# Block transposes on VectorE and a regroup through DRAM in place of crossbar transposes, in a linear-attention and FP4 feed-forward layer

## Chip, core and metric

The kernel runs on one core of a Trainium2 chip. The time is device microseconds of that core for one launch; the reported figure is the median of 3 runs. The core has five engines with instruction queues of their own: TensorE (PE in the profile, with its weight loads as PEld), VectorE (DVE), ScalarE (ACT), GpSimd (POOL) and SyncE (SP), which here only issues DMAs. Each queue runs its instructions in order, and an instruction waits at the head of its queue until what it needs is there.

## The reference

One layer over x of shape (16, 512, 256), all in float32. First attention without a softmax over the sequence, with 16 heads of 16 features, then a gated feed-forward whose inputs and weights are quantised to FP4 in blocks of 16 and dequantised again. Both halves end with a residual and a LayerNorm.

```python
def features(x):                       # per head, last dim
    p = exp(x - max(x)); return p / (sum(p) + 1e-6)
q, k = features(x @ Wq + bq), features(x @ Wk + bk); v = x @ Wv + bv
context = (q @ k.T / (sum(q) + 1e-6)) @ v          # per batch and head
x = layernorm(x + context @ Wo + bo)

def fp4(x):                            # blocks of 16 along the last dim
    scale = maximum(max(abs(x)) / 6, 1e-12)
    return GRID[searchsorted(MID, abs(x / scale))] * sign(x) * scale
gate, up = fp4(x) @ fp4(w_gate).T, fp4(x) @ fp4(w_up).T       # w_gate, w_up: (704, 256)
x = layernorm(x + fp4(silu(gate) * up) @ fp4(w_down).T)       # w_down: (256, 704)
```

Since nothing but a division stands between q @ k.T and v, the kernel computes k.T @ v per batch, multiplies it with Wo to a 256x256 matrix M, and takes q @ M.

## The kernel before

P is 128, D is 256, FF is 704. A batch has four tiles of 128 tokens, taken as two pairs; there are 32 pairs. The body does not run its work as it is written. Every operation is entered in a `Plan` with an engine, a time, a due time and the buffers it reads and writes; `Plan.order` then simulates the engines and gives one order, and the instructions are issued in it. So the order on each queue comes from the planner's times (`t_pe`, `t_dve`, `t_act`, `t_pool`, lines 245 to 262, and for a DMA an issue time of 0.45 us unless told otherwise), from the due times (in units of PAIR = 25) and from the number of buffers of each tag. On the chip, each queue keeps that order whatever the real times are.

The work of a batch, in order:

- `load_x` (371) loads x. `split_x` (743), from batch 2 (EARLY) on, also loads x transposed: a crossbar DMA transposes the batch as 16-bit halves (748) into `xTr`, and four DMAs regroup it into planes `xpl` (754).
- `project` (758) gets xT of a pair either by four TensorE transposes and a ScalarE copy out of PSUM (`transposed`, 625, lines 632 and 635, batches 0 and 1) or by two ScalarE copies that join the 16-bit planes (`join`, 776). Then q and k (783) and v (793) are multiplied, VectorE adds the biases (786, 799) and takes the maxima (805), GpSimd subtracts them (809).
- `features` (813): exp on ScalarE (820), sums and reciprocals on VectorE (822 to 833), the product on GpSimd (839).
- `key_values` (843): k.T v (852) and M (866).
- `attend` (878): q is transposed by TensorE (632), the product with M (894), residual and LayerNorm (`norm`, 685), the result x1 to DRAM (905).

The second half works on pairs:

- `quantise` (909) loads x1 (912), `codes` (638) makes 16-bit codes `xc` and scales `ns_x` on VectorE and ScalarE (650 to 663). A crossbar DMA on the SP queue transposes the codes (923) into `xcT`. `spread_scales` (667) transposes the scales by TensorE (672), copies them (674), writes them to DRAM by a DMA on ScalarE's queue (677) and reads them back on the SP queue so that every partition has the scale of its block of 16 (681). GpSimd multiplies both to `xqT` (928).
- `gate_up` (932): per tile, gate and up in two halves of 352 columns (948), silu on ScalarE (953), the product on VectorE (955), `codes` again, then for the pair a crossbar DMA of the codes `hc` (987), `spread_scales`, and GpSimd's products into `hq` (991). The columns of `w_guT` are laid out with the last 64 rows twice, so that the two tiles of a pair share the middle of eleven groups of 128. The last pair is dequantised by VectorE and transposed by TensorE instead (960 to 985).
- `down` (995): six products of 256 columns per tile (1005), residual, LayerNorm, output.

Every float32 product is two instructions in the profile, a transpose is one. The buffers that hold `hq` and the spread scales of h ("big") are two. `weight_scales` and `fp4_exact` (476, 518) quantise the weights, spread between the first batches; `transpose_gate_up` and `transpose_down` (568, 593) transpose them by TensorE. `due_at` (1019) puts the first half LEAD = 11 batches ahead of the second: the first gate of pair 0 is due when the attention of eleven batches is.

## Time and profile before

| what | us |
|---|---|
| median of 3 runs | 796.67 (795.27 to 798.91) |
| the profiled execution | 797.62 |
| its span, first to last instruction | 795.9 |
| ScalarE busy with the joins of x (L776, 56 of 0.762) | 39.1 |
| ScalarE busy with copies of scales (L674, 63) | 16.2 |
| GpSimd busy with products into hq (L991, 31 of 1.658 and 31 of 1.421) | 95.4 |
| GpSimd busy with products into xqT (L928, 32 of 1.168) | 37.4 |
| GpSimd waiting for the read of h's scales before L991 | 114.4 |

TensorE's granted clock is 0.996 over the span. The DMA engines moved 100.68 MB in 141884 packets, 95069 of them under 512 bytes. Of the time of 16 DMA engines, SP's queue (q1) took 55.3%, ScalarE's (q10) 7.5%. The landing times of DMAs are not given for this run, so they are read from the instruction that waited for one.

The times in these views are of one execution. "Busy" of an engine is the union of its instructions' spans; the times of lines can overlap a little. In the timeline, the columns are start, length, engine, line, operation, tile written and tile read, and the number of instructions merged; a queue's name ends in q. An issue of a DMA is the time that its queue is held, not the transfer.

### The profile page before, as it was taken

To read this page: it belongs to the slowest core of one execution; us is meant where nothing else is said; L and a number is where in the kernel's file an instruction comes from. 1 tells how busy PE (TensorE), PEld (TensorE's weight loads), DVE (VectorE), ACT (ScalarE), POOL (GpSimd) and SP (SyncE) were. 2 spreads that over 40 slices of the span, in tenths; PEclk is the share of its full clock that TensorE was granted. 3 is DMA by queue.
4 is the path that set the end of the run, shared out by engine and by line. 5 is a ranking of instruction groups with operands and counts; after the bars stand their busy time and mean duration, and the time that the engine had idled before them with its cause. 6 is when DMAs were issued, how large, how long until landed. Compare 5 with 4: busy or idle time off the path is not lost.

```text
span 795.9 us, 10225 instructions
## 1 busy us (share of the span) xinstructions
PE 770.2 (97%) x3134; PEld 550.4 (69%) x3134; DVE 589.4 (74%) x1194; ACT 441.5 (55%) x978; POOL 413.4 (52%) x510
## 2 busy tenths in 40 slices
PE   7999999998989999999999999999999999999996
PEld 4575766675766767777777777777777777677775
DVE  3979988887788798677666776776776776776663
ACT  1385786756879976545555444444444444444432
POOL 3488886978798766554533333343343343343331
PEclk9999999999999999999999999999999999999999
DMA  9536463434343243594374978977977977977721
GB/s 271 129 97 180 126 167 90 124 98 132 92 133 93 67 116 90 133 117 114 89 132 137 131 145 140 140 136 139 144 135 139 139 138 139 143 141 140 132 70 41
DMA packets 141884, 100.68 MB, mean 126 GB/s; under 512 B 95069, under 2 KB 125317, under 8 KB 141829
## 3 DMA queue, kind: packets, MB, share of 16 engines
q1 hardware_dynamic: 123464, 80.53, 55.3%
q10 hardware_dynamic: 18365, 19.49, 7.5%
q8 instruction: 25, 0.41, 0.2%
q14 instruction: 30, 0.25, 0.1%
HBM read 51.25 MB, written 18.70 MB: 88 GB/s over the span
## 4 chain that ended last, share of the span: by engine, by line
PE 83%; DVE 10%; ACT 3%; DMA 2%; POOL 1%; issue 1%; POOLq 0%; SPq 0%; DVEq 0%; ACTq 0%
PE bank L948 37%; PE bank L1005 20%; PE bank L783 10%; PE bank L894 6%; PE bank L793 4%; PE bank L852 2%; DVE fs L822 2%; PE bank L866 1%; PE bank L632 1%; DVE qk L786 1%; DVE mx L805 1%; DVE fr L833 1%; DMA x<-dx 1%; PE bank L672 1%; ACT qk L820 1%
## 5 line engine op out<-in xcount | busy, mean ns | idle before, releaser
L948 PE MATMUL bank<-w_guT,xqT 128*128 128x352 f32 x1024 | 310.6, 459 | 0.0
L948 PEld LDWEIGHTS bank<-w_guT,xqT 128*128 128x128 f32 x1024 | 193.9, 190 | 101.9 <-issue 1.4
L1005 PE MATMUL bank<-w_dT,hq 128*128 128x256 f32 x768 | 174.3, 379 | 0.6 <-DVE r L695 0.6
L991 POOL TENSOR_TENSOR hq<-hcT,hq 128x768 f32<-128x768 bf16 (+1 forms) x62 | 94.1, 1539 | 133.1 <-DMA hq<-d_h 114.4
L1005 PEld LDWEIGHTS bank<-w_dT,hq 128*128 128x128 f32 x768 | 141.9, 190 | 25.2 <-issue 4.2
L955 DVE TENSOR_TENSOR h<-bank,g 128x352 f32<-128x352 f32 x128 | 66.7, 522 | 93.0 <-PE bank L948 53.5
L783 PE MATMUL bank<-w_qkv,xT 128*128 128x512 f32 x256 | 123.4, 611 | 6.2 <-DVE qk L786 3.1
L953 ACT ACTIVATE g<-bank 128x352 f32<-128x352 f32 x128 | 58.6, 460 | 96.7 <-PE bank L948 94.4
L809 POOL TENSOR_TENSOR qk<-qk,mx 128x512 f32<-128x512 f32 x64 | 67.5, 1077 | 31.9 <-DVE mx L805 31.8
L783 PEld LDWEIGHTS bank<-w_qkv,xT 128*128 128x128 f32 x256 | 47.7, 196 | 48.5 <-issue 33.8
L839 POOL TENSOR_TENSOR qk<-qk,fr 128x512 f32<-128x512 f32 x64 | 66.5, 1067 | 23.2 <-DVE fr L833 12.1
L661 ACT ACTIVATE sq<-h,magic 128x704 f32<-128x704 uint16 x64 | 56.4, 881 | 29.2 <-DVE h L658 28.3
L723 POOL TENSOR_SCALAR var_d<-var_d 128x2 f32<-128x2 f32 x31 | 5.9, 191 | 120.6 <-ACT y L719 120.5
L786 DVE TENSOR_TENSOR qk<-bank,b_qkv 128x512 f32<-128x512 f32 x64 | 43.4, 682 | 32.4 <-PE bank L783 31.9
L793 PE MATMUL bank<-w_qkv,xT 128*128 128x256 f32 x256 | 60.7, 380 | 1.6 <-DVE v L799 1.2
L894 PE MATMUL bank<-M,qT 128*128 128x256 f32 x256 | 59.8, 381 | 1.5 <-ACT M L872 1.3
L793 PEld LDWEIGHTS bank<-w_qkv,xT 128*128 128x128 f32 x256 | 48.0, 190 | 16.7 <-issue 8.1
L650 DVE TENSOR_REDUCE bank<-h 128x44 f32<-128x704 f32 x64 | 57.3, 895 | 2.0
L658 DVE SCALAR_TENSOR_TENSOR h<-h,bank 128x704 f32<-128x704 f32 x64 | 56.7, 886 | 2.1
L894 PEld LDWEIGHTS bank<-M,qT 128*128 128x128 f32 x256 | 48.2, 190 | 13.7 <-issue 3.4
L887 POOL TENSOR_TENSOR xb<-x,b_o 128x512 f32<-128x512 f32 x32 | 41.0, 1284 | 20.8 <-DVE r L710 20.2
L674 ACT COPY sT_h<-bank 88x128 f32<-88x128 f32 x31 | 8.1, 260 | 73.6 <-PE bank L672 65.0
(139 smaller groups left out, 1081.5 us busy)
## 6 DMA issues: line engine op xcount, KB each, us to landing
hq<-d_h SPq DMA_DIRECT2D x31, 704.0 KB
dx<-x1n ACTq DMA_DIRECT2D x32, 256.0 KB
x<-dx SPq DMA_DIRECT2D x32, 256.0 KB
xs<-d_x SPq DMA_DIRECT2D x32, 256.0 KB
out_dram<-y ACTq DMA_DIRECT2D x31, 256.0 KB
x<-_attn_hidden_states_dram SPq DMA_DIRECT2D x15, 512.0 KB
xpl<-xTr SPq DMA_DIRECT2D x56, 128.0 KB
d_h<-sT_h ACTq DMA_DIRECT2D x31, 44.0 KB
```

The costliest lines, as they stand in the source:

```text
L650: op("DVE", t_dve(n), due, lambda: nc.vector.tensor_reduce(amax[:, g], b3(src()), AX.X, ALU.max, apply_absolute_value=True), ins=[src_b], ...
L658: op("DVE", t_dve(n), due, lambda: nc.vector.scalar_tensor_tensor(b3(xn()), b3(src()), TIE * UP / BIG, bcast(inv[:, g], BLK), ALU.mult, AL ...
L783: op("PE", t_pe(D2), due, lambda c=c, u=u, pqk=pqk: nc.tensor.matmul(pqk.tile, xT[:, 2 * c + u, :], w_qkv[:, c, :D2], start=c == 0, stop=c ...
L793: nc.tensor.matmul(pv[:, u * D : (u + 1) * D], xT[:, 2 * c + u, :], w_qkv[:, c, D2:], start=c == 0, stop=c == DC - 1,)
L809: op("POOL", t_pool(D2), due, lambda g=g: nc.gpsimd.tensor_tensor(qk3()[:, g, :], qk3()[:, g, :], bcast(mx[:, g], HD), ALU.subtract), ins= ...
L839: nc.gpsimd.tensor_tensor(f3, f3, bcast(r[:, t * 2 * H : (t + 1) * 2 * H], HD), ALU.mult)
L894: nc.tensor.matmul(pu(pa.tile)[:, u, :], qT[:, 2 * u + c, :], M[:, c, :], start=c == 0, stop=c == DC - 1,)
L948: op("PE", t_pe(F2), due + u * 0.2 * PAIR, lambda c=c, u=u, lo=lo, ps_=ps_: nc.tensor.matmul(ps_[:, :F2], xqT[:, 2 * u + c, :], w_guT[:, c ...
L953: op("ACT", t_act(F2), due, lambda g=g, pg=pg: nc.scalar.activation(g.tile, pg[:, :F2], AF.Silu), ins=[pg], outs=[g], table="silu")
L955: op("DVE", t_dve(F2), due, lambda g=g, h=h, pu_=pu_, k=k: nc.vector.tensor_tensor(h[:, k * F2 : (k + 1) * F2], pu_[:, :F2], g.tile, ALU.m ...
L991: op("POOL", t_pool((gs.stop - gs.start) * P), d, lambda gs=gs: nc.gpsimd.tensor_tensor(part(1)[:, gs, :], hcT[:, gs, :], part(0)[:, gs, : ...
L1005: op("PE", t_pe(D), due, lambda f=f, g=g, u=u: nc.tensor.matmul(pu(pd.tile)[:, u, :], part(1)[:, g, :], w_dT[:, f + u * (f == NR), :], sta ...
```

## The change

- **Codes.** Before, one crossbar DMA turns codes of 128 tokens by n into their transpose. After, two neighbouring 16-bit codes are taken as one 32-bit word, VectorE transposes blocks of 32 by 32 words, one write puts the tile into DRAM and four reads, one for each 32 partitions, bring the blocks back so that a partition holds two neighbouring features for all tokens (`regroup`). All five DMAs are on the SP queue. Even and odd features lie side by side, so `w_guT` and `w_dT` are transposed from every second column, and GpSimd reads every second code. h has its codes padded from 704 to 768 per tile, in two fixed slots that are cleared at the start.
- **Scales.** VectorE transposes them in blocks of 32, four DMAs on the SP queue write them, one reads them back for every partition. TensorE's transposes, ScalarE's copies and the writes on ScalarE's queue go.
- **x.** TensorE transposes x in all batches; `split_x` and the joins go.
- **Order.** LEAD is 10; x has four buffers and its loads are all due six intervals ahead; weights are due one interval earlier, those of `w_down` two; gates from pair 2 on wait for `w_dT`. The last pair's route is the same with a layout of its own (12 transposes instead of 11). The maxima and reciprocals for x have one slot each instead of two.

```diff
-LEAD = 11
-
-EARLY = 2
+LEAD = 10
+
+FIRST = 2
...
-    FX = FF + TR
+    TG = -(-FF // (2 * P))
+    LW = FF // 2 - (TG - 1) * P
+    HB = 2 * P // BLK
...
-    places = {"amx": [0, 0], "ivx": [2 * D // BLK * 2, 0], "amh": [2 * D // BLK * 4, 0]}
-    places["ivh"] = [places["amh"][0] + 2 * FF // BLK * 2, 0]
+    slots, places = {"amx": 1, "ivx": 1, "amh": 2, "ivh": 2, "ivd": 1}, {}
+    for tag, k in slots.items():
+        places[tag] = [sum(slots[t] * 2 * (D if t[2] == "x" else FF) // BLK for t in places), 0]
...
+    nsh = const.tile([P, 2, 2 * TG * HB], F32, name="nsh")
+    hcs = const.tile([P, 2, 2 * TG * 2 * P], U16, name="hcs")
...
-        x = buf([TPB, D], "x", 3, f"x_{b}")
+        x = buf([TPB, D], "x", 4, f"x_{b}")
...
-    w_guT = const.tile([P, DC, 2 * FX], F32, name="w_guT")
-
-    w_dT = const.tile([P, NR + 2, D], F32, name="w_dT")
+    w_guT = const.tile([P, DC, 2 * FF], F32, name="w_guT")
+
+    w_dT = const.tile([P, 2 * TG, D], F32, name="w_dT")
...
+        nc.gpsimd.memset(nsh, 0.0)
+        nc.gpsimd.memset(hcs, 0.0)
...
-                        nc.tensor.transpose(pt[:, j, :], gu_rows()[:, r, cols], ident)
+                        nc.tensor.transpose(pt[:, j, :], gu_rows()[:, r, c::2], ident)
...
+                        at = 2 * P * g + t
+                        nc.tensor.transpose(pt[:n, 2 * t + c, :], dn_rows()[:, c, at : at + 2 * n - 1 : 2], ident)
...
-    def spread_scales(nscale, nb, dst, tag, name, due, holds=()):
-
-        n = P // BLK
-        pt = psum("pt", f"ps{name}")
-        sT = buf([P], "sT" + tag, 2, f"sT_{name}")
-        op("PE", t_pe(P) / 2, due, lambda: nc.tensor.transpose(pt[:nb, 0, :], nscale[:, :nb], ident),
-           ins=[nscale], outs=[pt], holds=[sT])
-        op("ACT", t_act(P) + 0.05, due, lambda: nc.scalar.copy(sT[:nb, :], pt[:nb, 0, :]), ins=[pt], outs=[sT])
-
-        d = Buf(dr, [n, nb // n, P], "d" + tag, 3, f"d_{name}")
-        dma(f"w{name}", 4.0, due, lambda: nc.scalar.dma_start(d.tile.rearrange("b g t -> g b t"), sT[:nb, :]),
-            ins=[sT], outs=[d], queue="ACT")
+    def regroup(src, dst, n, tag, name, due):
+
+
+        d = Buf(dr, [P, 4, n], "g" + tag, 3, f"g_{name}", U32)
+        dma(f"g{name}", 3.0, due, lambda: nc.sync.dma_start(d.tile, src.tile), ins=[src], outs=[d])
+
+        def back():
+            rows = d.tile.rearrange("(a i) q n -> i a q n", i=32)
+            for q in range(4):
+                nc.sync.dma_start(dst[32 * q : 32 * q + 32, :, :], rows[:, :, q, :])
+
+        dma(f"h{name}", 3.5, due, back, ins=[d], outs=[dst], issue=1.8)
+
+    def spread_scales(nscale, G, dst, tag, name, due, holds=()):
+
+
+        n = P // 8
+
+        sT = buf([G, 32], "sT" + tag, 2, f"sT_{name}")
+        op("DVE", 0.15 + 32 * G / 960.0, due, lambda: nc.vector.transpose(
+            sT.tile.rearrange("p g (r u) -> p g r u", u=2),
+            nscale.tile.rearrange("p (u g r) -> p g r u", u=2, r=n),
+        ), ins=[nscale], outs=[sT], port=True)
+        d = Buf(dr, [2 * n, G, P], "d" + tag, 3, f"d_{name}")
+
+        def write():
+            for a in range(0, P, 32):
+                nc.sync.dma_start(d[:, :, a : a + 32], sT[a : a + 32, :, :])
+
+        dma(f"w{name}", 4.0, due, write, ins=[sT], outs=[d], issue=1.8)
         into, dst_b = dst
 
-        dma(f"r{name}", 4.0 + nb * 0.08, due, lambda: nc.sync.dma_start(
-            into(), d.tile.rearrange("b g t -> b (g t)").unsqueeze(1).to_broadcast([n, BLK, nb // n * P])),
+        dma(f"r{name}", 3.0 + 0.7 * G, due, lambda: nc.sync.dma_start(
+            into(), d.tile.rearrange("(r u) g t -> r (u g t)", u=2).unsqueeze(1).to_broadcast([n, 8, 2 * G * P])),
             ins=[d], outs=[dst_b], holds=holds)
...
-    def split_x(b, due):
-
-
-        t = buf([2 * DC, L], "xTr", 1, f"xTr_{b}", U16)
-        pl = planes[b] = buf([2, DC, L], "xpl", 1, f"xpl_{b}", U16)
-        dma(f"xt{b}", 8.0, due, lambda: nc.sync.dma_start_transpose(t.tile, hidden[b].bitcast(U16)),
-            outs=[t], issue=5.0)
-
-        def regroup():
-            for h in range(2):
-                for g in range(2):
-                    nc.sync.dma_start(pl[g * P // 2 : (g + 1) * P // 2, h, :, :], t[h:P:2, g::2, :])
-
-        dma(f"xg{b}", 4.0, due, regroup, ins=[t], outs=[pl], issue=1.8)
...
-        if b < EARLY:
-            xT = transposed(
-                lambda: [x[:, 2 * p + u, cc * P : (cc + 1) * P] for cc in range(DC) for u in range(2)],
-                "xT", f"xT_{n}", due, [x if b else (x, p)],
-            )
-        else:
-            xT, pl = buf([2 * DC, P], "xT", 2, f"xT_{n}"), planes[b]
-
-            def join():
-                for h in range(2):
-                    half = xT.tile.bitcast(U16).rearrange("p (c u) (n t) -> p c (u n) t", c=DC, t=2)[:, :, :, h]
-                    nc.scalar.copy(half, pl[:, h, :, p * 2 * P : (p + 1) * 2 * P])
-
-            op("ACT", 2 * (0.16 + 2 * D / 975.0), due, join, ins=[pl], outs=[xT], name="join")
+        xT = transposed(
+            lambda: [x[:, 2 * p + u, cc * P : (cc + 1) * P] for cc in range(DC) for u in range(2)],
+            "xT", f"xT_{n}", due, [x if b else (x, p)],
+        )
...
-        xcT = buf([G, P], "xcT", 2, f"xcT_{i}", BF16)
-        dma(f"xT{i}", 4.0, due, lambda: nc.sync.dma_start_transpose(xcT.tile, xc.tile.bitcast(BF16)),
-            ins=[xc], outs=[xcT], issue=1.2)
-        xs_ = buf([G, P], "xs", 2, f"xs_{i}")
-        xqT = buf([G, P], "xqT", 2, f"xqT_{i}")
-        spread_scales(scales[1], n // BLK, (lambda: xs_.tile.rearrange("p g t -> p (g t)"), xs_), "x", f"x{i}", due, [xqT])
-        op("POOL", t_pool(n), due, lambda: nc.gpsimd.tensor_tensor(xqT.tile, xcT.tile, xs_.tile, ALU.mult),
-           ins=[xcT, xs_], outs=[xqT])
+        xw, xcT = (buf([4, 2 * 32], t, 2, f"{t}_{i}", U32) for t in ("xw", "xcT"))
+        op("DVE", 0.15 + n / 2 / 960.0, due, lambda: nc.vector.transpose(
+            xw.tile.rearrange("p q (u t) -> p q u t", u=2),
+            xc.tile.bitcast(U32).rearrange("p (u q t) -> p q u t", u=2, q=4)), ins=[xc], outs=[xw], port=True)
+        regroup(xw, xcT, 2 * 32, "x", f"x{i}", due)
+        xs_ = buf([2 * P], "xs", 2, f"xs_{i}")
+        xqT = buf([2 * DC, P], "xqT", 2, f"xqT_{i}")
+        spread_scales(scales[1], 1, (lambda: xs_.tile, xs_), "x", f"x{i}", due, [xqT])
+        for u in range(2):
+            op("POOL", t_pool(D), due, lambda u=u: nc.gpsimd.tensor_tensor(
+                xqT[:, DC * u : DC * (u + 1), :].rearrange("p c (a t) -> p c a t", t=32),
+                xcT.tile.bitcast(BF16).rearrange("p a (u t c) -> p u c a t", u=2, c=2)[:, u],
+                xs_[:, u * P : (u + 1) * P].rearrange("p (a t) -> p a t", t=32).unsqueeze(1).to_broadcast([P, DC, 4, 32]),
+                ALU.mult,
+            ), ins=[xcT, xs_], outs=[(xqT, u)])
...
-        scales = am, buf([2 * FF // BLK], "nsh", 2, f"ns_h{i}"), iv
-        hc = buf([2 * FF], "hc", 2, f"hc_{i}", U16)
+        scales = am, Slot("nsh", f"ns_h{i}"), iv
+        hc = Slot("hc", f"hc_{i}")
         both = big(f"hq_{i}")
-        part = lambda j: both[:, j, :].rearrange("p (g t) -> p g t", t=P)
-        s["h"] = both, part
+        flat = lambda: both.tile.rearrange("p a b -> p (a b)")
+        NQ = 2 * 2 * TG * P
+
+        hq = lambda: flat()[:, :NQ].rearrange("p (u g c t) -> p u g c t", u=2, g=TG, c=2)
+        hs = lambda: flat()[:, NQ : NQ + 2 * TG * P].rearrange("p (u g t) -> p u g t", u=2, g=TG)
+        s["h"] = both, hq
...
-                for ps_, off in ((pg, 0), (pu_, FX)):
+                for ps_, off in ((pg, 0), (pu_, FF)):
                     for c in range(DC):
-                        lo = off + (1 - u) * TR + k * F2
+                        lo = off + k * F2
...
-                        ), ins=[xqT, wguT_b[c]], outs=[ps_], holds=[h, sq], name="gate_up")
+                        ), ins=[(xqT, u), wguT_b[c]] + [wdT_b] * (i >= FIRST), outs=[ps_], holds=[h, sq], name="gate_up")
...
-            codes(of(h), of(h), of(sq), hc, u, FF, scales, u * FF, f"h{i}_{u}", due + (0.3 + 0.2 * u) * PAIR)
+            codes(of(h), of(h), of(sq), hc, u, FF, scales, u * TG * 2 * P, f"h{i}_{u}", due + (0.3 + 0.2 * u) * PAIR,
+                  u * TG * HB)
...
+                hd = buf([FF], "ff", NFF, f"hd_{i}_{u}")
...
-                        nc.tensor.transpose(pt[:, k, :], part(0)[:, g, :], ident)
...
+                                nc.tensor.transpose(pt[:n, 2 * m + c, :], hd[:, at : at + 2 * n - 1 : 2], ident)
...
-        hcT = buf([NG, P], "hcT", 2, f"hcT_{i}", BF16)
-        dma(f"hT{i}", 4.0, d, lambda: nc.sync.dma_start_transpose(hcT.tile, hc.tile.bitcast(BF16)),
-            ins=[hc], outs=[hcT], issue=4.0)
-        spread_scales(scales[1], 2 * FF // BLK, (lambda: both[:, 0, :], (both, "s")), "h", f"h{i}", d)
-        for j, gs in enumerate((slice(0, NR + 1), slice(NR + 1, NG))):
-            op("POOL", t_pool((gs.stop - gs.start) * P), d, lambda gs=gs: nc.gpsimd.tensor_tensor(
-                part(1)[:, gs, :], hcT[:, gs, :], part(0)[:, gs, :], ALU.mult
-            ), ins=[hcT, (both, "s")], outs=[(both, k) for k in (("0a", "0b", "mid"), ("1a", "1b"))[j]])
+        hw, hcT = (buf([4, 2 * TG * 32], t, 2, f"{t}_{i}", U32) for t in ("hw", "hcT"))
+        words = lambda: hc[:, :].bitcast(U32).rearrange("p (u g q t) -> p u q g t", u=2, g=TG, q=4)
+        for u in range(2):
+            op("DVE", 0.15 + TG * P / 960.0, d, lambda u=u: nc.vector.transpose(
+                hw.tile.rearrange("p q (u g t) -> p u q g t", u=2, g=TG)[:, u], words()[:, u]),
+               ins=[(hc, u)], outs=[(hw, u)], port=True)
+        regroup(hw, hcT, 2 * TG * 32, "h", f"h{i}", d)
+        spread_scales(scales[1], TG, (lambda: flat()[:, NQ : NQ + 2 * TG * P], (both, "s")), "h", f"h{i}", d)
+        for u in range(2):
+            for c in range(2):
+                op("POOL", t_pool(TG * P), d, lambda u=u, c=c: nc.gpsimd.tensor_tensor(
+                    hq()[:, u, :, c, :].rearrange("p g (a t) -> p g a t", t=32),
+                    hcT.tile.bitcast(BF16).rearrange("p a (u g t c) -> p u c g a t", u=2, g=TG, c=2)[:, u, c],
+                    hs()[:, u, :, :].rearrange("p g (a t) -> p g a t", t=32), ALU.mult,
+                ), ins=[hcT, (both, "s")], outs=[(both, f"{u}{c}{j}") for j in range(2)])
...
-            for f in range(NR + 1):
-                g = NR if f == NR else f + u * (NR + 1)
-                op("PE", t_pe(D), due, lambda f=f, g=g, u=u: nc.tensor.matmul(
-                    pu(pd.tile)[:, u, :], part(1)[:, g, :], w_dT[:, f + u * (f == NR), :],
-                    start=f == 0, stop=f == NR,
-                ), ins=[(both, "mid" if f == NR else f"{u}b" if f == NR - 1 else f"{u}a"), wdT_b], outs=[(pd, u)], holds=[r], name="down")
+            for f in range(2 * TG):
+                g, c = divmod(f, 2)
+                n = P if g < TG - 1 else LW
+                op("PE", t_pe(D), due, lambda f=f, g=g, c=c, n=n, u=u: nc.tensor.matmul(
+                    pu(pd.tile)[:, u, :], hq()[:n, u, g, c, :], w_dT[:n, f, :],
+                    start=f == 0, stop=f == 2 * TG - 1,
+                ), ins=[(both, f"{u}{c}{int(g == TG - 1)}"), wdT_b], outs=[(pd, u)], holds=[r], name="down")
...
-        load_x(b, d - (6 if b < EARLY + 1 else 3) * PAIR)
-        if b >= EARLY:
-            split_x(b, d - 6 * PAIR)
+        load_x(b, d - 6 * PAIR)
...
-    wdue = -2 * PAIR
+    wdue = -3 * PAIR
...
-    ddue = wdue + 2 * PAIR
+    ddue = wdue + PAIR
```

## The prediction

> **What bounds the kernel now.** I read the page's busy line first, then the chain that ended last.
>
> ```profile
> PE 770.2 (97%) x3134; PEld 550.4 (69%) x3134; DVE 589.4 (74%) x1194; ACT 441.5 (55%) x978; POOL 413.4 (52%) x510
> ...
> PE 83%; DVE 10%; ACT 3%; DMA 2%; POOL 1%; issue 1%; POOLq 0%; SPq 0%; DVEq 0%; ACTq 0%
> ```
>
> TensorE is busy nearly everywhere and holds 83% of the chain. Then the busy times by stretch, for the part in which only the second half of the layer is left (quantise, gate and up, down):
>
> ```profile
> 450.00:750.00 300.00, 300.00 (x1171) 215.72 (x1170) 214.29 (x457) 137.27 (x325) 104.70 (x122) 1.00 0.86 140
> ```
>
> The columns are length, then PE, PEld, DVE, ACT and POOL busy, granted clock, DMA share and GB/s. TensorE is busy for all 300 us at full clock; VectorE has 29% left. The chain of waits in this part shows one pair of token tiles:
>
> ```profile
> 508.63 9.47 PE bank L948 x32
> 518.09 0.11 PE bank L672
> 518.20 3.02 PE bank L1005 x14
> 521.23 0.11 PE bank L672
> 521.34 2.16 PE bank L1005 x10
> 523.50 9.47 PE bank L948 x32
> ```
>
> A pair takes 523.50 - 508.63 = 14.87 us: 9.47 of gate and up, 5.18 of down, 0.22 for two transposes of scales. Nothing but the stream of matmuls is on the path. Last, the issues of the SP queue over one such pair, in order of time:
>
> ```profile
> 506.40 0.60 SPq L681 DMA_DIRECT2D xs<-d_x  x1
> 508.99 1.43 SPq L987 DMA_TRANSPOSE hcT<-hc  x1
> 510.65 0.60 SPq L681 DMA_DIRECT2D hq<-d_h  x1
> 511.35 1.19 SPq L923 DMA_TRANSPOSE xcT<-xc  x1
> 512.60 0.57 SPq L912 DMA_DIRECT2D x<-dx  x1
> 520.87 0.61 SPq L681 DMA_DIRECT2D xs<-d_x  x1
> ```
>
> Five DMAs, 4.4 us of issue in 14.87. The queue is idle two thirds of the time, so its order costs nothing.
>
> **TensorE work.** Removed: 32 + 31 transposes of scales (L672) at 0.11 us in the chain, 6.9 us. Added: the x transposes of 14 batches, 2 pairs x 4 = 8 each, 112 instructions. The same operation stands in the chain before as groups of four q transposes:
>
> ```profile
> 50.03 0.44 PE bank L632 x4
> ```
>
> That is 28 x 0.44 = 12.3 us. Down keeps 12 products of 256 columns per pair (24 instructions), two of them per tile over 96 rows instead of 128; I price these the same, since the matmul rows are alike for a given number of columns. One transpose more in the last pair is 0.1. Net +5.4 us, if TensorE stays full.
>
> **ScalarE.** Removed: 56 half copies of x (L776) at 0.762, 42.7 us, and 63 copies of transposed scales at 0.26, 16 us, as well as two DMA issues a pair on its queue (0.64 and 0.80). Added: 28 copies of PSUM to xT at 0.588, 16.5 us. It is idle 45% of the span; I take no gain from this outside the first rival.
>
> **GpSimd.** One multiply of 512 (1.168) becomes two of 256, and two of 768 and 640 (1.658 and 1.421) become four of 384. The slope is (1.658 - 1.421) / 128 = 1.85 ns an element, the rest 0.24; so 2 x 0.71 + 4 x 0.95 = 5.2 us a pair instead of 4.25. Codes are now read every second element; at twice the time it would be 10.5, plus 1.1 for the norm, still under 14.66. In the trace the h multiply ends at 522 and the down that uses it starts at 533, so 11 us cover the longer chain. The two larger memsets at the start (512 elements took 0.53, so about 3 us) lie in 13 us of idle GpSimd in the first 20 us, behind the identity that the first transposes need.
>
> **VectorE.** Added per pair: a block transpose of x codes (256 words per partition), two of h codes (384 each), scales of 32 and 96. No row shows this operation. A low bound is the row of the code shift, 0.545 for 704 elements; a high bound is twice the float row, 0.52 for 352 and 0.89 for 704, which gives 0.16 + 1.03 ns an element. With that row: 0.42 + 2 x 0.55 + 0.19 + 0.26 = 1.97 us. Ends 1.0 and 3.9; I take 1.97, the row of the same word size. VectorE needs 214.29 x 14.87 / 300 = 10.6 us a pair now, so 12.6 (11.6 to 14.5) against 14.66. It is nearly filled but does not pass TensorE.
>
> The Trainium skill (VectorE: DVE Perf Modes, The three transpose paths) gives 311 ns for VectorE's 128x128 in bf16 and 1309 ns for the DMA crossbar. By that, 2.4 ns an element, a pair's block transposes would be estimated at 2.8 us and VectorE at 13.4, still under TensorE. The same section recommends the crossbar over a plain copy that reorders by strides, which speaks against regrouping through DRAM; in this trace the crossbar is an issue of 1.19 or 1.43 us.
>
> **The SP queue, which decides.** The change takes two crossbar issues off it and puts on: one write and four reads for the regrouped x codes, four writes and one read for their scales, the same ten for h; with the x1 load 21 DMAs a pair. Scale writes also move here from ScalarE's queue. A regroup in four DMAs exists before, for x:
>
> ```profile
> 132.49 2.57 SPq L754 DMA_DIRECT2D xpl<-xTr  x4
> ...
> 137.92 1.95 SPq L748 DMA_TRANSPOSE xTr<-_attn_hidden_states_dram  x1
> ```
>
> So 0.64 us each. Sixteen in groups are 10.3 us, five single ones at 0.60 and a gap of 0.07 are 3.35: 13.6 us of issue a pair, against 14.66 of TensorE. The planner counts 0.45 each, 9.5 us, and places them by that. What is left for waits is 1.1 us. But SP works in order, and each regroup's reads must wait until its write has landed. The second line above waits for the four DMAs: 137.92 - 135.06 = 2.86 us after the last issue. If nothing stands between, SP loses that twice a pair. The codes of h and of x are ready close together (the crossbar for h starts at 508.99, x codes end at 509.9), so I expect the write of x codes (0.67) between, and one landing of 2.2 us uncovered, the other hidden under h's four reads. That makes 13.6 + 2.2 = 15.8 us a pair. Behind the waiting reads stand the scale reads and the next x1 load; GpSimd's multiplies wait for these, TensorE for the multiplies. Bounds: 13.6 with all covered, which is hidden under 14.66; 13.6 + 2 x 2.86 = 19.3 with none.
>
> It decides only where no attention work is left. In the mixed part a pair has 14.66 plus half a batch of attention, (16 x 0.43 + 32 x 0.216 + 1.78 + 0.86 + 16 x 0.11) / 2 = 9.1 us, so 23.8 against 19.3. With ten batches ahead, six batches or 12 pairs are mixed, 20 remain.
>
> **The front.** The x loads now come 6 intervals early with four buffers, weights are due one or two intervals earlier, the gate of pair 2 waits for w_down. The same VectorE work (24.24 of 25 us busy from 25 to 50 us) precedes the first gate; I take 0, between -8 and +8, some two thirds of the 12.7 us in which TensorE is idle between 20 and 300 us (the stretches' busy times).
>
> DMA engines: 0.86 busy in the stretch shown. The change drops the crossbar and cuts the scale reads from 704 to 384 KB and from 256 to 128 KB per pair, and adds 128 + 128 + 384 + 384 KB of regrouping; I take no bound from them.
>
> **Sum**, against the profiled execution's 797.62 (span 795.9, 0.95 above the median of 796.67): x transposes +12.3; 12 mixed pairs at -0.22, -2.6; 20 pairs at 15.8 - 14.87 = +0.93, +18.6. Together +28.3, 825.9, and 825 beside the median.
>
> **Rivals.**
> 1. Faster, by ScalarE's relief in the front: about 26 us less of copies and the end of the crossbar chain (GpSimd waited 10.9 us once at L839 for xT). If nearly all of the 12.7 us of front idle time goes, and SP's waits are all covered, 797 + 5.4 - 12 = 790. It decides from 9.4 us saved on (5.4 plus 4). Against it: the chain through these stalls is mainly VectorE (fs, mx, fr, weights), which loses no work.
> 2. SP fits: waits under 1.1 us a pair. Then TensorE's +5.4 is all: 802, with the front's bounds 794 to 810. For it: SP's idle 7.7 us a pair now is spread so that others fill it. Against it: 1.1 us is less than half a landing.
> 3. VectorE becomes the bound: block transposes at 3.9 us and port conflicts with GpSimd add 1.5; 16 us a pair, 20 x 1.1 + 9.7 = 829. Against it: 3.9 needs twice the float row.
>
> **Chances.** SP bound 0.56 (807 to 868); SP fits 0.27; faster 0.12; VectorE 0.05. From the bounds, 19.3 a pair would be 797 + 9.7 + 20 x 4.4 = 895, which needs both landings bare; I end the range at 868 (18 us a pair). Low end 796, to take in SP fits. A measurement here tells 0.5%, 4 us, from no change: of SP fits half lies within it. Faster 0.11, same 0.14, slower 0.75.
>
> **What would show it.** Right: in 500 to 700 us a pair over 15 us, TensorE busy below 97%, SP issuing without idle except before the regroup reads, their wait on the regroup write; transposes of x at 0.44 per four; VectorE under 90%. Wrong: a pair of 14.66 with TensorE full (rival 2), VectorE above 97% (rival 3), the first gate far earlier than 264 us with fewer TensorE gaps (rival 1). A DMA issue of 0.4 us for these shapes would undo my price for SP.

## The result, and the profile after

The change takes 802.62 us (median of 13 runs, 798.02 to 805.37); the kernel before, run beside it, 796.32 (13 runs, 795.16 to 799.01). The ratio is 1.0068, 95% interval 1.0049 to 1.0087: slower, by 6.3 us, where 28 were forecast. The profiled execution took 802.72 with a span of 801.0, beside 797.62 and 795.9 before: 5.1 us of span to explain.

The page of the changed kernel, its busy line and the chain that ended last, by engine:

```profile
PE 776.3 (97%) x3182; PEld 561.2 (70%) x3182; DVE 639.2 (80%) x1350; ACT 410.1 (51%) x884; POOL 456.2 (57%) x603
...
PE 66%; POOL 13%; DMA 7%; issue 4%; ACT 3%; DVE 3%; SPq 3%; ACTq 0%; DVEq 0%; POOLq 0%
```

TensorE is busy 6.1 us longer than before, and idle 24.7 us instead of 25.7. So the difference is time in which TensorE is busy (more work, and work at a lower clock), not waiting, taken over the whole. By stretches it is less even. After, with the columns length, PE, PEld, DVE, ACT, POOL, clock, DMA share, GB/s:

```profile
20.00:300.00 280.00, 272.63 (x1202) 193.67 (x1202) 244.32 (x472) 182.59 (x383) 218.29 (x267) 1.00 0.23 70
...
450.00:750.00 300.00, 300.00 (x1150) 217.53 (x1149) 247.88 (x560) 130.77 (x296) 129.36 (x184) 1.00 0.51 145
...
770.00:780.00 10.00, 5.84 (x25) 4.40 (x24) 7.60 (x16) 3.04 (x5) 3.60 (x3) 0.87 0.36 106
780.00:790.00 10.00, 10.00 (x41) 8.51 (x39) 1.20 (x5) 4.17 (x13) 2.09 (x5) 0.78 0.07 26
```

The same stretches of the kernel before, except the long one, which the prediction shows:

```profile
20.00:300.00 280.00, 267.32 (x1135) 185.63 (x1133) 238.31 (x450) 205.07 (x431) 217.33 (x266) 0.99 0.45 118
...
770.00:780.00 10.00, 8.80 (x45) 7.27 (x44) 7.78 (x16) 2.96 (x10) 3.01 (x2) 1.00 0.04 15
780.00:790.00 10.00, 9.36 (x43) 7.57 (x41) 1.98 (x9) 3.63 (x11) 2.69 (x7) 1.00 0.14 46
```

Three things are to be seen. In the front TensorE's idle time fell from 280 - 267.32 = 12.7 us to 7.4. From 450 to 750 us it is full, as before: SP did not take over. At the end, from 770 on, there is new idle time and a lower clock. The chain in the part without attention confirms the middle one:

```profile
553.31 9.47 PE bank L955 x32
562.77 5.18 PE bank L1024 x24
567.96 9.47 PE bank L955 x32
```

A pair takes 567.96 - 553.31 = 14.65 us, 0.22 less than before, since the two scale transposes are gone. SP's queue over one pair explains why it does not bind (each line: start, us, and the issues of one kind in a row; L676 and L681 are the regroup's write and reads, L699 and L704 the scales'):

```profile
573.82 0.53 SPq L676 DMA_DIRECT2D g_h<-hw  x1
574.45 0.38 SPq L908 DMA_DIRECT2D x<-dx  x1
574.92 0.43 SPq L676 DMA_DIRECT2D g_x<-xw  x1
575.47 1.99 SPq L699 DMA_DIRECT2D d_x<-sT_x  x4
577.56 4.44 SPq L681 DMA_DIRECT2D hcT<-g_h  x4
582.10 0.54 SPq L704 DMA_DIRECT2D hq<-d_h  x1
582.74 1.96 SPq L681 DMA_DIRECT2D xcT<-g_x  x4
584.74 0.54 SPq L704 DMA_DIRECT2D xs<-d_x  x1
585.38 2.49 SPq L699 DMA_DIRECT2D d_h<-sT_h  x4
```

All 21 DMAs are there. The durations of a single issue, over the whole run (min/median/max in ns), are in the views of three of the lines:

```profile
L681 SPq DMA_DIRECT2D hcT<-g_h x124: 302/430/1176, 263.4 to 771.9; - x124
...
L676 SPq DMA_DIRECT2D g_h<-hw x31: 326/376/533, 259.2 to 766.1; - x31
...
L699 SPq DMA_DIRECT2D d_h<-sT_h x124: 549/596/1482, 254.5 to 765.4; - x124
```

With 0.43 for the eight reads, 0.38 for the two writes of codes, 0.60 and 0.42 for the four writes each of h's and x's scales, 0.54 for the two broadcast reads and 0.52 for x1, a pair's 21 issues are 9.9 us, with gaps of 0.06 some 11.1. And between the write of h's codes (573.82) and their reads (577.56) stand 3.2 us of other issues; the page gives 2.8 us as the write's median landing. In this pair nothing of it is bare, and in all of 450 to 750 us SP waits 3.4 us for such a write of h.

The four reads take 4.44 instead of the 1.8 of four in a row: SP waits inside them. The largest wait of its queue from 450 to 750 us (waiting line, what it waited for, us in total, times, longest) is

```profile
SPq L681 <- DMA out_dram<-y: 51.7, 16, 5.4
```

`out_dram<-y` is the write of the finished output, issued on ScalarE's queue. It shares no data with the reads. But every DMA of this program signals its landing on one of eight semaphores, which the DMAs of both queues take in turn, and before it is issued it waits for the last DMA that used the same one. In the pair shown the third read waits for semaphore 102, last used by the output's write, which landed at 581.21; the read is issued at 581.22. So 2.5 of the 14.65 - 11.1 = 3.5 us a pair that SP has beyond its issues go into waiting for another queue's DMA. They cost nothing here, since TensorE stays full.

The tail is where time was lost. The chain there (start, us, what):

```profile
763.53 0.56 SPq L699
...
765.41 0.60 SPq L699
766.10 4.43 DMA g_h<-hw
...
772.45 3.83 DMA hq<-d_h
...
776.40 1.76 POOL hq L1007
778.21 2.07 PE bank L1024 x4
...
781.56 8.79 PE bank L1024 x34
```

The last pair is transposed by TensorE, but pair 30 still goes through DRAM, and by now no gate work is left to cover it: the last gate ends at 768.0. Its codes wait behind four scale writes, land after 4.43 us, the scale read takes 3.83 more, and pair 30's `down` starts at 778.21. TensorE's own waits show a second late path (columns as for SP's waits):

```profile
PE bank L989 <- ACT sq L666: 3.2, 1, 3.2
...
PE bank L1024 <- POOL hq L1007: 1.0, 1, 1.0
```

L989 is the transposes of the last pair. The first of them stand ahead of pair 30's `down` and start at 775.85, just after VectorE has dequantised the first tile (775.7) and ScalarE has done its step on the second (L666, 775.8); only the last 1.0 us is spent on pair 30's products. Both paths are late by about the same: an earlier pair 30 alone would have taken off at most the last 1.0 of these 4.2 us of waiting. From the last gate to the end it is 33.0 us; before it was 25.1 (770.8 to 795.9). Part of that is the clock (same columns as the stretches):

```profile
777.80:780.20 2.40, 1.99 (x5) 1.52 (x6) 0.61 (x4) 0.04 (x1) 2.40 (x4) 0.50 0.00 0
780.20:783.60 3.40, 3.40 (x13) 2.90 (x12) 0.42 (x1) 1.78 (x6) 1.26 (x3) 0.50 0.00 0
```

After the idle time the granted clock is 0.50 until 784.2, some 6.8 us in all. So the 5.1 us are +7.9 in the tail and -2.8 ahead of it. There 12.3 us of x transposes came; 6.9 of scale transposes, 5.3 of front idle time and 1.7 of half clock (one stretch of 3.4 us in the front of the kernel before, none there now) went; that makes -1.6, and the rest of 1.2 is not assigned.

### The profile page after: what moved, and what is told of

Same layout as the page of the kernel before. It is cut to its first block, busy times and chain, and to the rows that moved or that the text cites. A ratio compares the mean times of both kernels' runs of the same rounds, so it can differ in the third digit from the quotient of the medians.

```text
span 801.0 us, 11076 instructions
## 1 busy us (share of the span) xinstructions
PE 776.3 (97%) x3182; PEld 561.2 (70%) x3182; DVE 639.2 (80%) x1350; ACT 410.1 (51%) x884; POOL 456.2 (57%) x603
## 4 chain that ended last, share of the span: by engine, by line
PE 66%; POOL 13%; DMA 7%; issue 4%; ACT 3%; DVE 3%; SPq 3%; ACTq 0%; DVEq 0%; POOLq 0%
PE bank L955 25%; PE bank L1024 14%; PE bank L779 10%; PE bank L890 5%; PE bank L789 5%; DMA out_dram<-y 3%; POOL hq L1007 3%; PE bank L848 2%; PE bank L636 2%; POOL qk L805 2%; SPq L681 2%; POOL xqT L927 2%; POOL qk L835 2%; PE bank L862 1%; POOL xb L883 1%
## 5 line engine op out<-in xcount | busy, mean ns | idle before, releaser
L1007 POOL TENSOR_TENSOR hq<-hcT,hq 128x384 f32<-128x384 bf16 x124 | 124.9, 1039 | 206.5 <-DMA hcT<-g_h 70.2
L1024 PE MATMUL bank<-w_dT,hq 128*128 128x256 f32 (+1 forms) x768 | 175.4, 383 | 1.5 <-POOL hq L1007 1.0
L1024 PEld LDWEIGHTS bank<-w_dT,hq 128*128 128x128 f32 (+1 forms) x768 | 146.3, 192 | 26.1 <-POOL hq L1007 1.4
L779 PE MATMUL bank<-w_qkv,xT 128*128 128x512 f32 x256 | 119.7, 601 | 2.8 <-DVE r L733 2.0
L666 ACT ACTIVATE sq<-h,magic 128x704 f32<-128x704 uint16 x64 | 56.3, 879 | 81.5 <-DVE h L663 80.3
L779 PEld LDWEIGHTS bank<-w_qkv,xT 128*128 128x128 f32 x256 | 47.4, 193 | 45.0 <-issue 36.2
L805 POOL TENSOR_TENSOR qk<-qk,mx 128x512 f32<-128x512 f32 x64 | 68.3, 1090 | 15.4 <-DVE mx L801 15.3
L755 ACT ACTIVATE y<-r,nb_d,rstd_d 128x256 f32<-128x256 f32 x62 | 33.8, 592 | 76.0 <-POOL nb_d L748 76.0
L927 POOL TENSOR_TENSOR xqT<-xcT,xs 128x256 f32<-128x256 bf16 x64 | 46.0, 737 | 13.4 <-DMA d_h<-sT_h 11.1
L668 DVE TENSOR_SCALAR hcs<-sq 128x704 uint16<-128x704 uint16 x64 | 39.3, 615 | 8.8 <-ACT sq L666 8.6
```

Source lines behind the costliest of these rows:

```text
L779: op("PE", t_pe(D2), due, lambda c=c, u=u, pqk=pqk: nc.tensor.matmul(pqk.tile, xT[:, 2 * c + u, :], w_qkv[:, c, :D2], start=c == 0, stop=c ...
L805: op("POOL", t_pool(D2), due, lambda g=g: nc.gpsimd.tensor_tensor(qk3()[:, g, :], qk3()[:, g, :], bcast(mx[:, g], HD), ALU.subtract), ins= ...
L927: op("POOL", t_pool(D), due, lambda u=u: nc.gpsimd.tensor_tensor(xqT[:, DC * u : DC * (u + 1), :].rearrange("p c (a t) -> p c a t", t=32), ...
L1007: op("POOL", t_pool(TG * P), d, lambda u=u, c=c: nc.gpsimd.tensor_tensor(hq()[:, u, :, c, :].rearrange("p g (a t) -> p g a t", t=32), hcT. ...
L1024: op("PE", t_pe(D), due, lambda f=f, g=g, c=c, n=n, u=u: nc.tensor.matmul(pu(pd.tile)[:, u, :], hq()[:n, u, g, c, :], w_dT[:n, f, :], star ...
```

## The experiments

Ratios are to the kernel before on the same chip. The groups of edits are called X (x transposed by TensorE in all batches), C (codes and scales in blocks, regrouped through DRAM) and O (the order: ten batches ahead, four buffers for x, x and weights due earlier, gates wait for w_down).

**X alone (e2_x_only).** On the kernel before:

```diff
-EARLY = 2
+EARLY = 16
```

> The kernel before, with x transposed by TensorE in all batches, nothing else of the change. Work theory: 112 transposes at 0.11 us on a full TensorE, +12.3: 808 to 809. Front theory: the crossbar chain for x and the two ScalarE joins a pair had cost TensorE idle time in the front, about 8 us of which goes with them: 799 to 803, with TensorE idle under 8 us between 20 and 300 us (12.7 before).

810.07, ratio 1.0176 (1.0154 to 1.0198), +13.8, above both expectations. The 12.3 us of transposes are paid in full, and more: front idle time falls only to 8.6, and the mixed part gets new idle time, since TensorE, which still transposes scales there, waits for VectorE's scales and products (150 - 145.25 = 4.75 us):

```profile
300.00:450.00 150.00, 145.25 (x607) 106.20 (x606) 102.09 (x208) 76.52 (x173) 66.95 (x82) 1.00 0.49 104
```

**C with O, without X (e3_codes_only).** On the changed kernel, with `split_x` and `join` of before back for batches 2 and up:

```diff
+EARLY = 2
...
-        x = buf([TPB, D], "x", 4, f"x_{b}")
+        x = buf([TPB, D], "x", 3, f"x_{b}")
...
-        load_x(b, d - 6 * PAIR)
+        load_x(b, d - (6 if b < EARLY + 1 else 3) * PAIR)
+        if b >= EARLY:
+            split_x(b, d - 6 * PAIR)
```

> The changed kernel with x again by the crossbar from batch 2 on (x buffers and load times as before). Work theory: 12.3 us less of TensorE work, 802.6 - 12.3 = 790. Front theory: about 8 us of idle time between 20 and 300 us come back, 797 to 800.

802.16, ratio 1.0084 (1.006 to 1.0108), above both expectations and no faster than the whole change, although 12.3 us of TensorE work are gone. So X is not a plain cost once C is there.

**O alone (e5_order_only), and X with O (e6_x_and_order).** On the kernel before; the second with EARLY = 16 as well:

```diff
-LEAD = 11
+LEAD = 10
+FIRST = 2
...
-                        ), ins=[xqT, wguT_b[c]], outs=[ps_], holds=[h, sq], name="gate_up")
+                        ), ins=[xqT, wguT_b[c]] + [wdT_b] * (i >= FIRST), outs=[ps_], holds=[h, sq], name="gate_up")
...
-    wdue = -2 * PAIR
+    wdue = -3 * PAIR
-    ddue = wdue + 2 * PAIR
+    ddue = wdue + PAIR
```

> The kernel before with only the order of the change: LEAD 10, four x buffers loaded six intervals ahead, weights due earlier, gates from pair 2 on after w_down's transposes. Theory A (the order is what makes room for x on TensorE): 796 to 799 alone, since no work is added. Theory B (the order costs time of its own in the front): 800 to 804.

> The kernel before with x by TensorE in all batches and the order of the change; codes by the crossbar, scales by TensorE as before. Theory A: the order takes the stalls out that x alone left between 300 and 450 us (4.7 us of idle TensorE): 803 to 806. Theory B: as x alone or worse, 809 to 814.

808.38, ratio 1.0163 (1.0148 to 1.0177), and 821.9, ratio 1.0327 (1.031 to 1.0344). Both are above every expectation. Without C the order of the change costs 12.6 us, and it adds to X. The first of TensorE's waits in e5 is

```profile
PE bank L674 <- DVE ns_h L656: 6.8, 3, 3.2
```

and 9.1 us in e6, 0.4 in the kernel before: a scale transpose (L674 here) at the head of TensorE's queue, its scales late from VectorE, and the matmuls behind it wait too. That is 6.8 of the 12.6 us in e5; 4.7 us more are a wait for GpSimd. C takes these transposes off TensorE, and with them this wait; that this is why O costs little beside C is inferred, not tested by itself.

**C without O (e7_codes_no_order), and X and C without O (e8_x_codes_no_order).** Both undo O on the changed kernel; the first has `split_x` and `join` back as in e3:

```diff
-LEAD = 10
+LEAD = 11
-FIRST = 2
+FIRST = 99
...
-    wdue = -3 * PAIR
+    wdue = -2 * PAIR
-    ddue = wdue + PAIR
+    ddue = wdue + 2 * PAIR
```

> The changed kernel with x by the crossbar and the order of before: only the blocks by VectorE and the regroup through DRAM are left of the change. By TensorE's work -6.9 us, by the tail +8: 797 to 799 if nothing else moves (theory A). If codes through VectorE and SP disturb the front by themselves (theory B), TensorE's granted clock is below 0.994 and the time 801 to 805 as with the order.

> The changed kernel with the order of before (LEAD 11, three x buffers, weights due later). Theory A: x costs its full work again, 808 to 812. Theory B (order is worth nothing, what offsets x's work is the shorter code path): 801 to 804.

805.69, ratio 1.0118 (1.0105 to 1.0131), just above its second expectation, and 800.13, ratio 1.0058 (1.004 to 1.0075). Adding X made the kernel 5.6 us faster, where the expectations for e8 began at 801. The front of e7 shows how: TensorE is idle for 19.2 us there, and the clock of 200 to 300 us is 0.93, two stretches of 6.8 us at half clock. In e8 it is 7.4 us and one stretch of 3.4. That outweighs the 12.3 us of transposes. The largest wait of e7 is that of TensorE's line for q and k, L808 here (idle us and releaser at the end):

```profile
L808 PE MATMUL bank<-w_qkv,xT 128*128 128x512 f32 x256 | 127.6, 627 | 15.4 <-ACT xT L801 11.8 <-ACT M L897 1.5 <-DVE qk L811 1.1
```

TensorE waits for the joins of x (L801), 7.5 us at the longest. SP's queue has a long wait near the same place:

```profile
SPq L683 <- POOL xqT L956: 26.7, 2, 17.3
```

```profile
242.94 2.56 SPq L779 DMA_DIRECT2D xpl<-xTr  x4
...
285.55 1.82 SPq L683 DMA_DIRECT2D xcT<-g_x  x4
289.46 2.57 SPq L779 DMA_DIRECT2D xpl<-xTr  x4
```

The reads of x codes stand at the head of SP's queue for 17.3 us (268.2 to 285.5), until GpSimd frees their buffer, and behind them stands the regroup of the x planes of a later batch (L779). It is tempting to call that the cause, but the times do not allow it. The joins that end TensorE's wait run from 288.1 on and read planes that were issued at 242.94 and had landed at 248.3, before SP's wait began; and there is one plane buffer, so the regroup at 289.46 could not have gone before these joins were done. The chain ahead of them is

```profile
287.11 0.44 DVE wxm_d L582
287.57 0.56 ACT bank L583
288.13 1.31 ACT xT L801 x2
289.48 5.81 PE bank L808 x8
```

L582 and L583 quantise the weights. The joins stand behind them in ScalarE's queue, and these behind VectorE; the next longest wait, 3.9 us at 236.3, looks the same. So what the crossbar route of x cost beside C is joins that come late in ScalarE's order. Why the planner's order has them later in e7 than in the kernel before is not shown.

The eight corners, that is every combination of X, O and C, as ratios: none 1, X 1.0176, O 1.0163, XO 1.0327, C 1.0118, XC 1.0058, CO 1.0084, XCO (the change) 1.0068. X costs 1.6 to 1.8% without C; with C it gains 0.6% or, with O, nothing that can be told. O costs 1.5 to 1.6% without C; with X and C its effect lies within the intervals.

**Eight more reads on SP (e4_reads_in_8).** Each regroup read is split in two, 29 issues a pair instead of 21, the same bytes:

```diff
-                nc.sync.dma_start(dst[32 * q : 32 * q + 32, :, :], rows[:, :, q, :])
+                for a in range(0, 4, 2):
+                    nc.sync.dma_start(dst[32 * q : 32 * q + 32, a : a + 2, :], rows[:, a : a + 2, q, :])
```

> The changed kernel with each regroup's reads in eight DMAs instead of four, same bytes: 29 instead of 21 issues a pair on the SP queue. At the measured 0.43 us and a gap of 0.06 the queue's issue time goes from 11.2 to about 15.1 us a pair. SP theory (the queue would bound as I forecast, only its issues are cheaper): over 14.65, so the pairs without attention work take 15 to 17 us, 810 to 850 in all. Rival (the queue's issue time does not matter at all because reads overlap): 14.65 a pair, 801 to 805.

856.71, ratio 1.0762 (1.0738 to 1.0785), a little above the range expected. TensorE is no longer full:

```profile
450.00:750.00 300.00, 274.93 (x1007) 192.80 (x1006) 213.49 (x489) 112.12 (x255) 112.00 (x159) 0.97 0.44 126
```

56 instructions are a pair (32 and 24), so 1007 are 18 pairs, 16.7 us each. SP's queue:

```profile
609.97 4.46 SPq L682 DMA_DIRECT2D hcT<-g_h  x8
614.52 0.54 SPq L705 DMA_DIRECT2D hq<-d_h  x1
615.16 3.82 SPq L682 DMA_DIRECT2D xcT<-g_x  x8
...
626.50 7.37 SPq L682 DMA_DIRECT2D hcT<-g_h  x8
```

Eight reads are still 3.8 us of issue; with the rest of the round and its gaps 15.3 us are issue, the other 1.4 waits, most of them for the output's write again (20.2 us in the 300). So SP is the next bound, and it lies at most (14.65 - 11.1) / 0.53 = 6 or 7 issues away, fewer as far as its waits stay.

**h's codes ahead of its scales (e12_codes_first).** The tail shows codes behind four scale writes. Here the scale writes wait until the block transposes of the codes are done, so that the planner puts them behind:

```diff
-        dma(f"w{name}", 4.0, due, write, ins=[sT], outs=[d], issue=1.8)
+        dma(f"w{name}", 4.0, due, write, ins=[sT, *after], outs=[d], issue=1.8)
...
-        spread_scales(scales[1], TG, (lambda: flat()[:, NQ : NQ + 2 * TG * P], (both, "s")), "h", f"h{i}", d)
+        spread_scales(scales[1], TG, (lambda: flat()[:, NQ : NQ + 2 * TG * P], (both, "s")), "h", f"h{i}", d, after=[hw])
```

> The changed kernel with one edge more for the planner: the four scale writes of h wait until the block transposes of h's codes are done, so that the write of the codes goes ahead of them on the SP queue. Tail theory: pair 30's codes land some 2.5 us earlier at the end, so TensorE's wait before the products of pairs 30 and 31 shrinks: 2 to 4 us off, 798.5 to 800.5. If the tail sets nothing (work theory), or the scales become the late ones: 802 to 806.

825.41, ratio 1.0384 (1.0362 to 1.0407), far above both expectations, with the same 21 issues:

```profile
450.00:750.00 300.00, 284.41 (x1065) 199.40 (x1064) 230.55 (x522) 120.06 (x271) 123.28 (x171) 1.00 0.47 134
```

15.8 us a pair. SP's reads of h's codes over two pairs, and TensorE's first wait:

```profile
600.32 6.77 SPq L681 DMA_DIRECT2D hcT<-g_h  x4
...
617.68 6.04 SPq L681 DMA_DIRECT2D hcT<-g_h  x4
```

```profile
PE bank L1024 <- POOL hq L1007: 18.1, 30, 1.3
```

The read of h's scales stands behind these reads of codes, and now behind those of x's codes too; GpSimd's products wait for it, and TensorE waits for the products, 30 times. And the reads of codes themselves take 6 us and more, since the waits inside them for the output's write have grown from 51.7 to 71.0 us in 450 to 750. In e12's chain that write follows steps of its LayerNorm on GpSimd, which stand behind GpSimd's products, so the delay can feed itself. How much is the place of the scales and how much the shared semaphores no run separates. At the same 21 issues the order on SP is worth 23 us.

**The tail (e1_last2).** The last two pairs by TensorE instead of one:

```diff
-LAST = 1
+LAST = 2
```

> The changed kernel, with the last two pairs (instead of one) dequantised by VectorE and transposed by TensorE. Tail theory: of the 801.0 us span some 8 us are new idle time of TensorE after the last gate, in which it waits for pair 30's way through DRAM (writes, regroup, scale read, four GpSimd products). Then this edit takes 4 to 7 us off (12 more transposes cost 1.3): 796 to 799, and TensorE is busy for over 9 of the 10 us that follow the last gate. Work theory: the 6 us are the added x transposes, the tail is as before: 802 to 805.

802.31, ratio 1.007 (1.0049 to 1.0092): no change, where the tail's time should have come back. In its profile the tail is healed, 25.3 us from the last gate to the end, and no low clock up to the last product:

```profile
770.00:780.00 10.00, 10.00 (x50) 8.36 (x49) 8.25 (x17) 2.87 (x5) 0.00 (x0) 1.00 0.01 5
780.00:790.00 10.00, 9.48 (x45) 7.93 (x43) 2.38 (x9) 4.00 (x13) 2.14 (x6) 1.00 0.07 26
```

but the last gate ends at 772.6 instead of 768.0: 12 more transposes (1.3 us), 1 us of waiting ahead of them, and one stretch of half clock in the front, as in the kernel before, that the change's profile does not have. The profiled execution of e1 had a span of 797.9, 3.1 less than the change's, but it was the fastest of its six (799.6 to 804.04), and the median does not bear that out. The times go with the clock: e1's two fastest runs had 0.996 and 0.998, those above 802.5 had 0.992 to 0.994; in the change the two of 798.0 us had 0.996 and 0.997, the two above 804 had 0.991 and 0.993. Where the half clock lay in the slower runs no trace shows. What the tail costs is read from the trace, and was not shown as a gain in time.

**Scale writes on ScalarE's queue (e9_scales_on_act).** As before the change, but in four DMAs:

```diff
-                nc.sync.dma_start(d[:, :, a : a + 32], sT[a : a + 32, :, :])
+                nc.scalar.dma_start(d[:, :, a : a + 32], sT[a : a + 32, :, :])
...
-        dma(f"w{name}", 4.0, due, write, ins=[sT], outs=[d], issue=1.8)
+        dma(f"w{name}", 4.0, due, write, ins=[sT], outs=[d], issue=1.8, queue="ACT")
```

> The changed kernel with the four scale writes on ScalarE's DMA queue, as the one write was before: 13 instead of 21 issues a pair on SP. If SP fits already in the changed kernel, pairs without attention work stay at 14.65 us and only the tail gains (the write of pair 30's codes no longer stands behind four scale writes, 2.5 us): 799 to 802. If SP is what costs the 6 us (late products in single pairs): 795 to 798. If ScalarE's queue pays for the eight issues (3.5 us a pair): above 803.

806.07, ratio 1.0116 (1.0098 to 1.0133). TensorE is busy through all of 770 to 790 us, but waits 9.7 us in the front for copies of ScalarE:

```profile
L779 PE MATMUL bank<-w_qkv,xT 128*128 128x512 f32 x256 | 123.5, 612 | 9.7 <-ACT xT L639 9.7
```

The longest, 6.1 us at 224, ends a chain of norms and of weights being quantised in ScalarE's queue. No scale write was issued there in the 18 us before, so it is the order that changed; that the issues themselves delay these copies is not shown.

**Combinations (e10_no_order_last2, e11_no_order_last2_act).** e8 with LAST = 2, and that with the edit of e9:

```diff
-LAST = 1
+LAST = 2
```

> The version with codes and x of the change and the order of before (800.1), with the last two pairs transposed by TensorE. Its tail waits for pair 30's products less than that of the changed kernel does, so the edit takes 0 to 3 us: 797 to 800. As in e1, no gain if what the tail gives is paid back by 12 more transposes and the clock: 800 to 802.

> The same with the scale writes on ScalarE's queue too. If both help, 795 to 798; with SP no bound in either, the same as e10 within 1.5 us.

804.06, ratio 1.0092 (1.0076 to 1.0109), and 803.14, ratio 1.0082 (1.0067 to 1.0097): neither better than e8; e10 is above both its expectations, e11 within 1.5 us of it. In e10 TensorE is full from 770 to 790, but idle 3.9 us between 740 and 770 at a clock of 0.94: the wait has moved ahead of the last gates.

**x by the crossbar only while SP is free (e13_hybrid).** From e7: batches 2 to 8 by the crossbar, the rest by TensorE. The last plane leaves SP at 128 us, h's codes come there only after the first gate, at 266:

```diff
+LATE = 9
...
+        if not EARLY <= b < LATE:
+            xT = transposed(
...
+        if EARLY <= b < LATE:
+            split_x(b, d - 6 * PAIR)
```

> The codes of the change, the order of before, x by the crossbar in batches 2 to 8 only (SP carries no code blocks of h then) and by TensorE from batch 9 on. TensorE's work is 56 transposes or 6.2 us less than with x by TensorE everywhere and that order (800.1); the crossbar chain costs idle time again, 3 us by the rows of before between 20 and 200 us. Theory (the loss of e7 is the x planes queued behind codes on SP, which falls away here): 795 to 799. If the crossbar in the front itself brings the idle time and half-clock windows of e7: 803 to 806.

795.7 (794.75 to 799.75), ratio 1.0003 (0.9989 to 1.0018): level with the kernel before, the best version with C, and 10 us better than e7, as expected. That does not show the reason that was given for it, planes queued behind codes on SP: the late joins of e7 lie between 230 and 290 us, and there x goes by TensorE here. TensorE has 14 x 0.44 = 6.2 us of x transposes more than before and 6.9 of scale transposes less, and the front's idle time is 10.8 us. No version here beats the kernel before.

## Why the prediction was wrong

**The step that failed** is the price of the SP queue: "So 0.64 us each", 13.6 us of issue and "one landing of 2.2 us uncovered", 15.8 a pair. Measured are 0.47 a piece, 9.9 us and 11.1 with gaps, landings of h's codes bare for 3.4 us in 300, and a pair of 14.65 set by TensorE. So the 20 pairs give 20 x (14.65 - 14.87) = -4.4 us instead of +18.6. Two mistakes lie in it. The price was taken from the row nearest in purpose, the x planes' regroup (2.57 for four). In the changed kernel h's scale writes do take 0.60, but the reads over 32 partitions 0.43 and plain writes of 128 partitions 0.38. The issue time goes with the shape, and not with the bytes: 96 KB of h and 32 KB of x, both read over 32 partitions, take 0.43. And only one issue was placed between write and reads, where six stand, since x's scale writes and the x1 load come there too. The prediction had named the first mistake: "A DMA issue of 0.4 us for these shapes would undo my price for SP." The planner's 0.45, which it set aside, was nearer.

The Trainium skill (DMA: Bandwidth & Descriptors, Issuing engines are not separate DMA queues) says that a sequencer's time to start a DMA is usually small beside the DMA. For one DMA here it is, 0.43 against 2.4 us to landing; e4 shows that in sum it is not: eight more issues on SP cost 54 us.

**The mechanism** behind the failed term stands: SP in order, its issues and waits as the next bound, GpSimd and TensorE behind it. e4 shows it at 29 issues, e12 with one wait placed otherwise. In the change it is hidden. One part was not in the prediction: what SP waits for inside the reads is mostly not its own writes to land (3.4 us in 300 for h) but the output's write on the other queue (51.7).

**TensorE's work** was right: four x transposes are 0.44, a pair without scale transposes 14.65, +12.3 and -6.9. The second rival, SP fits, forecast 802 from this +5.4 alone. The time agrees, but the sum behind it does not: the front gave 5.3 us of idle time and 1.7 of clock (it was bounded by -8 and 8 and taken as 0), the tail took 7.9, and that these cancel is chance. The first rival needed more than 9.4 us from the front; it got these 7.0. The 7.7 us of SP's idle time in the second rival is the longest single gap of the lines shown; in all, 14.87 - 4.4 = 10.5 us a pair were idle.

**The tail was not in the sum.** "In the trace the h multiply ends at 522 and the down that uses it starts at 533, so 11 us cover the longer chain" was read in the middle. For pair 30, which has only the last pair's gate to cover it, the same chain is bare, as is the last pair's own route beside it. That the tail costs 7.9 us of the profiled span is read from the trace; e1 and e10 took it away and did not get faster, so why the time stays near 802 in them is not settled.

**The other terms.** VectorE's block transposes were put at 1.97 us a pair and are 0.44 + 2 x 0.57 + 0.18 + 0.24 = 2.00; the estimate of 2.8 beside it was too high, because it let the whole time of 128 elements grow with their number, where a part of some 0.15 us is fixed. The row of h's codes is

```profile
L1000 DVE STREAM_TRANSPOSE hw<-hcs 128x384 uint32<-128x384 uint32 x62 | 35.4, 573 | 1.1
```

VectorE is busy 247.88 of 300 us, 83%, where 86% was forecast, and does not bind. GpSimd's products are 4 x 1.04 + 2 x 0.74 = 5.6 us, put at 5.2. No term but SP's and the omitted tail was off by more than its bounds.

**X as a cost of 12.3 us** was right as work and wrong as a price in time: e7 and e8 show that with C, in the order of before, it gains 0.6%, since the idle time of the front and the half clock that follows it shrink by more than the transposes cost. That the parts could not be added was not thought of.

## What to carry to other kernels

Price a DMA issue by the row that is nearest in shape (partitions, pieces, direction), not in purpose, and write out the new order of the whole queue before calling a landing bare. A transfer that waits holds up everything behind it on an in-order queue, so ask of each what it waits for; the waits view names it, and it can be a DMA of another queue that shares nothing but a semaphore. Before you blame such a wait, check by the landing times that what stood behind it was needed earlier. And walk the new chain through the last pair, where nothing is left to cover it. When an edit has several parts, build the corners: here X cost 1.8% alone and gained 0.6% beside C.

## What the runs showed of the hardware

- A DMA issue on SP takes 0.38 us (128 partitions, plain write), 0.43 (32 partitions, read), 0.54 (broadcast read) or 0.60 (scale write of h), by its shape; halving the reads' bytes in e4 left their median at 0.425.
- The half-clock stretches came in lengths of about 3.4 or 6.8 us, each after idle time of TensorE: 6.8 in the tail of the change, 3.4 once in the front of the kernel before, 3.4, 6.8 and 3.4 in the front of e3, and none in e2. In the tail of the change products of 256 columns start 427 ns apart inside the stretch and 216 behind it, so full TensorE work takes twice as long, and a stretch costs 1.7 or 3.4 us. The Trainium skill (TensorE: Matmul & The Clock Gate, Part 1: The HAM clock gate) gives a free-running window of 3413 ns and half or full rate alone; the lengths and the 0.50 here agree.
- VectorE's block transpose of 32-bit words took 573, 438, 242 and 177 ns for 384, 256, 96 and 32 words a partition: near 0.15 us and 1.1 ns a word.
- Eight semaphores serve all DMAs of SP's and ScalarE's queues in turn in this program, and a DMA waits at the head of its queue until the last user of its semaphore has landed: SP waited 51.7 us from 450 to 750 us for ScalarE's output writes, 71.0 in e12.
